# Two-layer spectral attention block on one core: half turns, a 64-wide Gram, x fetched ahead, a new order

## The chip, the cores and the metric

The kernel runs on one core of one Trainium2 chip. The metric is the device time of one launch in microseconds (us), lower is better. The core's engines are TensorE (PE, with its weight loads as PEld), VectorE (DVE), ScalarE (ACT) and GpSimd (POOL), each with a program of its own that it works off strictly in order; SyncE (SP) issues the transfers. The engines wait for one another by semaphores. The work is in float32 throughout.

## What is computed

x has 2 images of 56 channels on a grid of 128 x 128. Two layers of the same form are applied, each with weights of its own. Cut to what matters:

```python
x = x + layer(gn(x))                      # twice; gn: group norm, 32 groups over the last axis
def layer(x):                             # x: 2 x 56 planes of 128 x 128
    xn = inorm(x)                         # mean and variance of each plane
    k, q, v = (fno(xn, W) for W in (K, Q, V))          # 1 -> 8 heads each
    attn = softmax(einsum(q, k) / sqrt(H * W))         # 56 x 56 for each head, over the planes
    out = fno(attn @ v, P)                             # 8 heads -> 1
    att = inorm(out + x);  an = inorm(att)
    h = gelu(inorm(spectral(an, M0)) + skip(an))
    h = inorm(spectral(h, M1)) + skip(h)
    return inorm(h) + att
def spectral(x, w):                       # rfft2, 32 x 16 lowest modes times w, irfft2
def fno(x, w): return spectral(x, w) + skip(x)         # skip: a 1 x 1 product
```

## The kernel before, in words

**Layout.** x lies in `X2`, one image's 56 planes on partitions 0 to 55 (one half of the rows) and 64 to 119 (the other half), with ones on the rows behind them that carry biases into products. For the Fourier transforms the image is turned: TensorE transposes bring a grid column onto the partitions (`turned`), copies put the result into `P[b]`, and `bn_stats` takes sums there. `b` is the image, 0 or 1; each image goes through all steps and both are interleaved.

**Steps of a layer.** `modes` works out the group norm's scale (`gs`, `gv`, `sh`: the statistics `mv` go through a product with `group`), scales `P[b]` in place, multiplies by the discrete Fourier matrix `fw`, turns blocks of 32 x 32 on DVE into `turns`, multiplies again and has the modes `xf`. `gram` multiplies `P[b]` with itself, 128 grid columns summed in PSUM, to a 56 x 56 matrix of all pixels (the skips' part of the scores). `scale_x` scales `X2` itself. `scores`, `softmax`, `values`, `mixes`, `heads` and `norms` are the attention, computed on modes with the products of the heads' weights, which `prepare` makes on the chip (raw weights in `xr`, through `relay` in DRAM, back as `tc16` and `tc20`) and `build` spreads into `WU` and `WT`, `build_m` into `WM`. `norms` ends with `inverse`, the first half of the transform back, to `Z`. `gelu` has 8 pieces of 16 rows for each image: `synthesis` (the second half of the transform) and `mixed` (the skips from `X2` by `Bs`) are summed in PSUM, ACT does Gelu and a Square with a sum, `turn_back` transposes on TensorE, `forward` multiplies by `fw`. `spectrum` is the second spectral product with its norms, a chain of short steps, again ending in `inverse`. `end` does `synthesis` and `mixed` with `Be`, a DVE step (stt) that adds the gelu's result, and adds the layer's input x, fetched again from DRAM into 3 slots of `xr` (`load`, `back`); it writes `store` (layer 0) or `out` (layer 1). For layer 0 it is followed by `turned` for layer 1.

**What sets the order.** The functions only record: each call of an engine becomes a unit of a `_Book`. `play` (lines 211 to 219) issues all units in an order written out by hand in a string, `_ORDER`; `_ENGINES` says for each unit which engine does it (DVE, POOL or ACT, where there is a choice) and `_BANKS` which of the 8 PSUM banks. So almost every instruction has line 218 in the profile, and groups are told by their tiles. SP's transfers, too, stand in that order and each waits at the head of its queue.

**What the change and the prediction touch.** `load_x`, `prepare`, `turned`, `sums` (used by `norms` and `spectrum`), `modes`, `gram`, `mixes`, `turn_back` in `gelu`, `end`, `play`, and the three strings. The Gram's loop before takes the 56 x 56 matrix in two pieces, in column tiles of 32, four of which take turns:

```python
u, v = 32 * (i % 4), 32 * ((i + 2) % 4)
mm(p[u : u + 32, :K], P[b][:, o : o + 32], P[b][:, o : o + K], i < 2, i >= N - 4, tile_position=(0, u))
mm(p[v : v + m, K : K + 28], P[b][:, o + 28 : o + 28 + m], P[b][:, o + 28 : o + K], ...)
```

Of the kernel before, what the change touches and what calls it, by code (L numbers as in the profile page):

```python
# [10 lines left out]
F32 = mybir.dt.float32  # L11
# [11 lines left out]
for _name, _n in (  # L23
    ("ident", N), ("fw", 32), ("group", N), ("raw", 56), ("fh", N), ("gw", N), ("ext", N), ("fold", 64),
    ("low", K), ("high", K), ("count", 2), ("syn", 1), ("same", 32), ("n2", 1), ("power", 1), ("fx", N), ("gh", 2 * N),
):
    _PARTS[_name] = (sum(n for _, n in _PARTS.values()), _n)
# [3 lines left out]
def _constants():  # L31
# [23 lines left out]
    group = (p[:, None] // 4 == p // 4) / 4.0  # L55
    k = np.arange(K)
    ext, fold = np.zeros((N, N)), np.zeros((N, 64))
    for r in range(2):
# [13 lines left out]
        [own, mirror, -mirror, count * dc * N * re, count * dc * N * im, dc * re, dc * im], 1  # L72
    ).reshape(N, 56)
# [6 lines left out]
        "count": np.concatenate([np.full((N, 1), 2.0), -1.0 * (edge2 & (ky2 != 16)[:, None])[:, :1]], 1),  # L80
        "syn": np.where(edge2 & (ky2 == 16)[:, None], 2.0, 1.0)[:, :1],
        "same": (ky2[:, None] == np.arange(32)) * 1.0,
        "low": ((p % 32)[:, None] == k) * (k < 28),
        "power": np.full((N, 1), -0.5),
        "high": ((p % 32)[:, None] + 28 == k) * (k >= 28),
# [3 lines left out]
    return {"all": np.ascontiguousarray(whole, np.float32), "one": np.ones((8, 64 * N), np.float32)}  # L89
# [79 lines left out]
class _Book:  # L169
# [40 lines left out]
    def play(self, order, chosen, at):  # L210
        for n in order:
            u = self.units[n]
            e = chosen.get(n, u.kind[0])
            for ways in u.calls:
                op, args, kw = ways[e]
                args = [self.to_ap(v, at) for v in args]
                kw = {k: self.to_ap(v, at) for k, v in kw.items()}
                getattr(self.engines[e], op)(*args, **kw)  # L218
# [11 lines left out]
def _planned(book):  # L230
# [8 lines left out]
    "734F05000s4s8q4p4K5m3X6l063U7I5h07080a090c0b0e0d0Z020V011011120W170f0X0Y1318031a19141b150p161f1c0l1d1e1g1j0h1h"  # L239
    "2C0i1i2z1n1k1m041l1Y1o210o201X220r1q2A0g1p0u0t0k0v0C1Z0F25233x280q3y240w3z260y270A0E3A3B293C0z2B2a2b3D2c2d0j3E"  # L240
    "3L3I2e2f3O2g3M2h3F2i0m3G3R3N3T3S0B0S0n0H0J0U0K0P8y0Q4x0M0O0I0N0R0L0D0T0x3H3P5O8x4y5N7b7a4z0G2D3Q4A2E2H9c4B2F2G"
    "2K4C2I2L2J4D2M2N2P2O4E2Q2S2R1r2T4G4H2U2V2W1H2X2Y1s2Z9b301v1I1u3J1t1w1J405P1D411x2k2l4V522j1L2p1K1E1z4W581M1G2w"
    "4T1A1N1O2y4U1P1C2q2v1y2m2u573K2x1T2n1Q2r1F4Z1B2t3d3V1R2s1U8C8z1S2o8A321W389e3W1V3c9g3e6i4I3Y4243398D4Y3Z446j3i"
    "4J3g3m3h314L343j3a5Q373o3b3n35335M5R3l5Y36454M4N46474O3f4X3k565U50484P495V4g4a3u5S3t4j5W4b4m3p5T6e4c4d5X3w4n4o"
    "4k5L5Z4v6f4e4l51604w4f5E3v4hir5x5A6g4i595J6hhB4q4Q3s5y3q4R4rgW6a4S5C614u7f626b4t633r5D7d645k556c5K7e5a6d5b5I65"
    "5c66677g685v7h695B6s8B8E5H6t8H5z8F6k5w8K6u6m6Y536r545F8G6p8I6v6q8L8J8M5G8N6E6n6w7k8O6ok26x5d6B6D6y6C5e6F6z5f6A"
    "8P9d8Q6G5g6H8S8R7l9f6K6J5i7c8T5j6I9j9k8U5l6L6M7m7i6N5n7x6Q7j6O6P796R998X7z6S968Y747n6W7591956T92986U8Z9476777B"
    "6V9093j36X787A8V5o5p975q9h5r7C6Z8W9i5s5t709o7y719a7F727D7G7E5u9V7oh17p7qa2h27rgYa97sa37t7uaah0i6h39Wh5gZa4h4ag"
    "9l9m9X7v9n9p9q7wah9r7P9s9t9u9w9v7Qai9x9y9z9A9B7R9C9D9Y7Sab9Z7T9Eadaca0aja1a5aedb7Ha6af8lddde7Ja7dg7Odfa8dhakdc"
    "an7U7Y807V7Zao7W8w827Xauap849Jal7M9Saravam9R7N81aw859Qas837K9Klp7Lax9Naq878688898a9TatayaB9I8c8b8d9O9M8eaC9G8g"  # L250
    "9F9L8faIaD8r8h8j8saz8vaJ8taF8i8u8kkKaAaKaG8oaE8m8paL9U9PbTaH8naM9HaNbYaOaPc5bJaQbKaWh6aRbMaXaTh7bLaYaUbNaSh8aZ"
    "bOh9bPb0aVbQb1bRbSb3b2bWb4bUbXb5bac0c6c7bVb6b7bZc1c2bbbhb8bobcc3c4c8c9cab9cbbpbdcccecdcfcgbqbebiclbjcmbrchcibl"
    "bkcncjckbfbmcqbgbscocrbnbtbucpbvbCbwbDdim7bxdjbydtdkbEbzdudobFbAcCdvdqbGbBdpejcHcOdxdldwesdmdnbHetdsekbIdreyct"
    "ezcveBdydDcudEdCdAdOeAdzcsdBelcwdFeCcxdPdJcyeDczdQdYdGdKcAdLeFdSe9dIcFcBdZdNdMeajsdRcGeGdHe0eHe1cDe2e3cJcEcPcQ"
    "eJcIe4dTcKeOe5eEe8eedVcLdUcMcNegcReKcScTePeIefcUdXcWcYe6cVcXeQdWcZe7eLeRd4d0d5ebeNeMd1eSedeceieud2eheTemf9imd6"
    "d3f8eUd7eVeneoepd9d8eqeWerdaf7f6gXeXfaeveZfbeYjvexflhEfcf5juf4fvewfmfGfgf0fHfnfifwfhf1hahbfQfpfxfofRf3g1fyfdgb"
    "f2fefAgcfBhefkhffSffgkfChdfFglhgfDfzfjhhfEgqhihjg2hkhygyfqhlhshmhzfshvhtgrfrhpftfugshnhugzhqhAfLhohwhHhxiefIfN"
    "hIfMifhrigiIfPihfJiHfKhCfOiLiGg3iiiChDg4ijg5gBhGjCipiNhFiKiAjxgdiFikjyilfTiPjziniojwfVgAjFfUjAiBiOjBfWiMjEjDfX"
    "fYiqg0jGgug6fZisitiuiviJgGgvjtg7gtgKg8gHgwgaiwjHg9iEgLgeixgJgIiyggiziDgCgfjIjJjKjVjLgNghjTgDgmpxpwgOgjjUjMpyiY"
    "jRjNjOgnpzgEgPgijPgxjQgSi9pukSkRjSpvgRgpk1gQgogTk9kFgFk3kagVjWgUk4kbgMk5hJk6jZk7hKhchLk0kljXhMhNhOhPhQi3k8hUi5"  # L260
    "hXi4hRhYi0hVhZhSjYhWi1hTkcici2kdiQiRidkejni7kikjjgkfi8kmibiSjjkgkkjciaknkhiTkqj1jmkoiUkWjfjokpjll2kXksjikrktjk"
    "iVjdiWkuiXjqkUkTiZkxj0kvkwjpjekykVkZkNkLkDkOkAj2kMjrkYkzj4kBl1kQj5l0l3kCl4j6j7kEkPj8j9jhjakIjbl5l6kGl7kJl8lile"
    "ljl9lmlalflbkHlclgldlklhlwlnlolxlqm2llmemlmfmmltlylulIlzmglrlAlvmnlsmhmilBlFlCmjlHlGmomdlDlEmklJmsmplLlKmzlOlN"
    "lMmtmAlPlQlRmqmBlUmClSlTmrmulVmDmvmwlWm8mGmxlXlYmHmalZm0m1mymImbm3m9mcmNmJm4mEmOm5mKmFm6mPmQmLmUmVmRmMmWmSn1mT"
    "mXmYn2n8mZnfn3n4ngn0n5ocn9nhohn6oonin7nao3njnco2nbo5nmo4nnndo6nonpneo7nko8nlnqo9oaobntnrofnuodognAojnvopoqoenH"
    "oiokolnBomnIonorosotounwnJovoxowoyoEozoFnKnxoAoBnCnsnyoCoDoGoJnLnzoHoKnDnEoInFnOnVqBnWqKnXqCqLrlrknPriqDrepArh"
    "nQrgpBrfnRrjpLpCqUqRpVqSpDqWpGq6qXpMpFpWpEpIq7qgpNpHpJqrpKpXpPqhpOqsoVr3nSr7pQnYqirar0nGp0pUp7nMpYnTq0nNnZnUpS"
    "o0pTq1o1pRoMq5q4oNq3pZoOq2oLrcr2oPr6q8r4q9oQqaoRr5qbrdqjqdqloSqfoToUqeoYqkqcqmoWoZqYrbp2oXp8p9qop1p3p4qpp5qqp6"
    "papbpcpdqnpepgpfphpnpipor8qwpjr1pkqZqtqxplpmpqqyqTpppsquprqzqvqEqAptqGqFr9qMrZqQqVs6qHrms7qJqIrts9qNqOs0ruqPs8"
    "rns1rwrzsasbrGs3s2rorAs5s4rvrqrMrBrxrNryrTrCrDrprsrUrErrrFrWrVrOrYrXrHrPrJrQrIrLrRrSrK"  # L270
)
_ENGINES = (
    "ADDDDDDDDDDDDDDDDDDDDDDDDDDDVGGGVGGVVGGGVGGVGVVVGVVGVGGVGPVVVPSVVPSVVPSVVPSVVPSVVPSVVPSVVPSVVPSVVPSVVPSVVPSVVP"
    "SVVPSVVPSVVVGVVGGGGVVGGGGVVGGGVVADDAADDAADDDDDDAAVGVGGGVVVGGGVVVGVVGVGVGGVGVDDADAADADADDDAADDVVVGGGVGVVVVVGVVV"
    "VPVVVGVVPVSPVVPVGPVVGGGPSGDDPSVVPVVVGVSPVSPVVPVGPVVGGGPVGDDPSPPPPPPPPGVSGPVSVVVGVPSGGGGVGGVGVVVVVGVPPPPPPPPGVV"
    "VPVSVVVGVPVGVVGVGVGGGVVGGGGGVGGGPSPSPPSPPVPVVVSVVVPSPSPSPSPSPSPVSPVPVPPPPPSVPSSVVGPVPVPVVVVGVVVPVVVVVVGPVPVVVV"
# [21 lines left out]
def fno_layers(ctx: ExitStack, tc: tile.TileContext, x, out, weights, small, const):  # L298
# [209 lines left out]
    def turned(b, g, L, stats):  # L508
# [17 lines left out]
        for s in range(2):  # L526
            V.bn_stats(stats[:, 2 * g + s, :], dst[:, 448 * s : 448 * s + 448])
# [593 lines left out]
```

## Time and profile before

| | us |
|---|---|
| three runs | 514.27, 510.6, 501.66 |
| median | 510.6 |
| profiled execution | 508.58 |
| its span, first to last instruction | 506.5 |
| busy in the span: PE, PEld | 383.8, 258.3 |
| DVE, ACT, POOL | 357.4, 174.7, 187.7 |
| mean granted TensorE clock | 0.902 |

The profile lists busy time by engine, the span in 40 equal slices (busy share in tenths, the clock that the throttle granted to TensorE in tenths, transfers), the chain of work that ended last, and groups of instructions. A group's line gives output and input by their names, their shapes, the count, busy us and the mean ns of one, and then the idle time of the engine before them and what ended it. "issue" as a releaser is time in which the engine waited for nothing that the profile shows. Matmuls are pipelined, so a mean duration of 0.2 us can go with a pace of tens of ns.

Marks of the stages in the trace before: statistics of the first image complete at 29.4 us, those of the second at 82.9; the first synthesis of layer 0's gelu part at 142.6; its end at 215.4; statistics of layer 1's first image at 265.0, of its second at 324.6; layer 1's gelu from 373.1 to 451.5; the last synthesis from 478.8; the last DVE step before 498.9, then transfers only. The functions of layer 1's first image that need `WU` begin at 284.4.

### The profile page before, as it was taken

The numbers are of one execution on the slowest core, as the hardware profiler recorded it, in microseconds if no ns is written. First come the engines' busy times: TensorE is split into PE (matmuls) and PEld (weight loads), VectorE is DVE, ScalarE is ACT, GpSimd is POOL, SyncE is SP. The second block draws the span as 40 slices with busy tenths as digits, with TensorE's granted clock in tenths as the row PEclk, the third lists the DMA queues.
The fourth block names the chain that finished last, engine by engine and source line by source line (L and its number), as shares of the span: only waits on it lengthen the run. The fifth ranks groups of instructions, "written<-read, shape, count | busy, mean of one in ns | idle before, by whom it ended". The sixth has DMA issues, their size and how long they took to land.

```text
span 506.5 us, 16657 instructions
## 1 busy us (share of the span) xinstructions
PE 383.8 (76%) x7408; PEld 258.3 (51%) x7408; DVE 357.4 (71%) x613; ACT 174.7 (34%) x238; POOL 187.7 (37%) x227
## 2 busy tenths in 40 slices
PE   2434465889899999995686696996999999954590
PEld 1414345368568656554543484756686546532340
DVE  2584299996685776599898859685756655685685
ACT  1410241521283768532003032620246677411000
POOL 0174097883142211144568634245201001113173
PEclk9999585999999999997798877988999999996696
DMA  8975620000002000146645144000000000378655
GB/s 185 235 149 97 138 47 8 1 20 5 14 3 63 7 2 2 39 137 204 214 116 178 32 132 145 3 12 5 3 3 2 1 1 3 105 224 236 191 170 185
DMA packets 27784, 42.00 MB, mean 83 GB/s; under 512 B 10272, under 2 KB 13216, under 8 KB 27680
## 3 DMA queue, kind: packets, MB, share of 16 engines
q1 hardware_dynamic: 25408, 40.49, 29.8%
q8 instruction: 58, 0.95, 0.8%
q10 hardware_dynamic: 2304, 0.44, 0.5%
q14 instruction: 14, 0.11, 0.1%
HBM read 25.48 MB, written 14.97 MB: 80 GB/s over the span
## 4 chain that ended last, share of the span: by engine, by line
PE 54%; DVE 24%; issue 8%; ACT 5%; POOL 3%; DVEq 0%; ACTq 0%; POOLq 0%
PE banks L218 54%; DVE P L218 8%; ACT P L218 3%; DVE WT L218 2%; DVE stats L218 2%; DVE X L218 2%; DVE WU L218 2%; DVE turns L218 1%; DVE dg L218 1%; DVE f L218 1%; DVE M L218 1%; DVE xr L218 1%; DVE vd L218 1%; DVE D L218 1%; DVE sh L218 1%
## 5 line engine op out<-in xcount | busy, mean ns | idle before, releaser
L218 ACT COPY P<-banks 128x896 f32<-128x896 f32 (+4 forms) x64 | 53.3, 856 | 141.8 <-PE banks L218 95.5
L218 PE MATMUL banks<-P 128*32 128x56 f32 (+3 forms) x2656 | 57.1, 220 | 21.7 <-issue 21.0
L218 PEld LDWEIGHTS banks<-P 128*32 128x32 f32 (+1 forms) x2656 | 48.7, 123 | 30.9 <-issue 27.0
L218 PE MATMUL banks<-C,P 32*128 32x128 f32 (+5 forms) x864 | 59.6, 274 | 3.2 <-DVE P L218 1.1
L218 PEld LDWEIGHTS banks<-C,P 32*128 32x128 f32 (+4 forms) x864 | 48.8, 167 | 22.1 <-issue 11.5
L218 POOL TENSOR_TENSOR X<-X,gvr 121x512 f32<-121x512 f32 x35 | 50.5, 1471 | 10.1 <-DVE gvr L218 7.2
L218 DVE SCALAR_TENSOR_TENSOR P<-P,hs,banks 128x1024 f32<-128x1024 f32 x32 | 39.8, 1275 | 14.7 <-PE banks L218 13.2
L218 DVE BATCH_NORM_STATS2 stats<-P 128x6 f32<-128x448 f32 x64 | 36.6, 611 | 18.7 <-ACT P L218 18.6
L218 PE MATMUL banks<-C,X 56*128 56x56 f32 (+1 forms) x384 | 33.0, 290 | 17.6 <-DMA X<-x 9.8
L218 POOL TENSOR_TENSOR X<-P,xr 128x512 f32<-128x512 f32 x22 | 29.3, 1347 | 32.0 <-DMA xr<-x 14.9
L218 ACT ACTIVATE P<-banks 128x1024 f32<-128x1024 f32 x32 | 32.0, 1021 | 22.5 <-PE banks L218 22.4
L218 PEld LDWEIGHTS banks<-C,X 56*128 56x128 f32 (+1 forms) x384 | 28.1, 181 | 22.7 <-issue 6.7
L218 PE MATMUL banks<-P,C 128*32 128x448 f32 (+2 forms) x216 | 29.8, 567 | 11.3 <-DVE P L218 6.2
L218 DVE TENSOR_TENSOR X<-X,gvr 121x512 f32<-121x512 f32 x29 | 32.8, 1157 | 0.8 <-ACT gvr L218 0.8
L218 ACT ACTIVATE banks<-P 128x1024 f32<-128x1024 f32 x32 | 32.9, 1027 | 0.7
L218 PE MATMUL banks<-X,Bs 57*64 57x512 f32 x256 | 33.0, 607 | 0.0
L218 PE MATMUL banks<-xf,WU 64*64 64x56 f32 x1024 | 24.1, 258 | 11.6 <-issue 6.0
L218 PE MATMUL banks<-X,BTx 57*64 57x512 f32 x256 | 32.5, 618 | 0.0
L218 PEld LDWEIGHTS banks<-xf,WU 64*64 64x64 f32 x1024 | 22.1, 170 | 13.8 <-issue 6.9
L218 PE MATMUL banks<-turns,C 128*32 128x224 f32 (+1 forms) x288 | 25.9, 395 | 4.2 <-DVE turns L218 2.9
L218 DVE COPY P<-banks 128x896 f32<-128x896 f32 (+4 forms) x16 | 14.8, 938 | 19.0 <-PE banks L218 19.0
L218 PEld LDWEIGHTS banks<-P,C 128*32 128x32 f32 (+2 forms) x216 | 11.2, 148 | 21.3 <-issue 8.4
(233 smaller groups left out, 645.1 us busy)
## 6 DMA issues: line engine op xcount, KB each, us to landing
X<-x SPq DMA_DIRECT2D x16, 448.0 KB
xr<-x SPq DMA_DIRECT2D x64, 112.0 KB
store<-X SPq DMA_DIRECT2D x32, 224.0 KB
out<-P SPq DMA_DIRECT2D x32, 224.0 KB
xr<-store SPq DMA_DIRECT2D x32, 112.0 KB
X<-store SPq DMA_DIRECT2D x32, 112.0 KB
X<-const_one SPq DMA_DIRECT2D x4, 256.0 KB
xr<-weights SPq DMA_DIRECT2D x4, 144.0 KB
```

The source lines that it names most:

```text
L218: getattr(self.engines[e], op)(*args, **kw)
```

## The change

1. **Turns.** All transposes are now of 56 rows, 16 in a group instead of 8 of 120 rows, and alternate between rows 0 to 55 and 64 to 119 (`turn`). In layer 0's first turns that was so already.
2. **Statistics.** `bn_stats` and `bn_aggr` on DVE go. The copy out of PSUM is an ACT activation with a running sum, and an ACT Square in place in PSUM gives the sum of squares; all 32 groups' copies are on ACT. The product with `group` now takes 16 columns, and one reduction follows.
3. **Gram** in pieces of 64 columns: 128 matmuls in two column tiles instead of 256 in four; one copy out instead of three.
4. **x for the ends** is fetched into 15 slots: 8 in `WU`, 4 in `WT`, 3 in `xr`. Loads of tile n + 15 follow the add of tile n. In the last end (layer 1, second image) x is added by TensorE, a product with the identity summed in PSUM, where POOL and DVE added it before. `WU` and `WT` of layer 1 can be built only when the tiles have been used.
5. **21 idle products** (`idle`) on TensorE that nothing reads: 17 of 128 x 512 and 4 of 128 x 256; 16 stand before and among the first turns.
6. **Ones** in `X2` come from memsets of rows 32 to 63 ahead of the loads of x and a one-row transfer, instead of four transfers of 256 KB.
7. **prepare** handles real and imaginary parts in one instruction, so has fewer and wider ones; all its transfers are on SP (before: SP or ACT).
8. **sums**: two DVE reductions and four matmuls become 18 matmuls of 32 columns, one copy and two small matmuls.
9. **mixes**: 8 matmuls to 128 rows become 16 to 64 rows in two column tiles.
10. **Order, engines, banks** are searched anew. In both layers syntheses of the first image's `end` that stood inside the gelu part now come behind it (two of four in layer 0, all four in layer 1), and the turns of the second image go between the first image's products. On SP, raw weights come ahead of x, and the prepared weights' write to DRAM ahead of the second image.

The core of the diff (the three strings and the constants' layout are left out):

```diff
     def play(self, order, chosen, at):
         for n in order:
+            if n >= len(self.units):
+                self.idle(n - len(self.units))
+                continue
...
+    slots = [t[:, 512 * n : 512 * n + 512] for t, k in ((WU, 8), (WT, 4), (xr, 3)) for n in range(k)]
...
     def load_x(b):
         for g in range(0, 8, 2):
+            fill("VG", X2[32:64, b, 8 * g : 8 * g + 16, :], 1.0)
...
-    for b in range(B):
-        for c in range(2):
-            D.dma_start(out=X2[64 * c + K : 64 * c + 64, b], in_=const["one"].rearrange("p (i w) -> p i w", w=N))
...
-        dma("DA", to, cpt)
+        D.dma_start(out=to, in_=cpt)
...
+    def turn(p, src):
+        for n in range(8):
+            for c in range(2):
+                q = slice(64 * c, 64 * c + K)
+                T.transpose(p[:, c, K * n : K * n + K], src(q, n), ident[q, q], tile_position=(64 * c, 0))
+
+    def turned(b, g, stats):
         p = pair()
...
-                    T.transpose(p[:, s, N * e : N * e + 120], X2[:120, b, i, :], ident[:120, :120])
+        turn(p, lambda q, n: X2[q, b, 8 * g + n, :])
         dst = P[b][:, 896 * g : 896 * g + 896]
...
-        for s in range(2):
-            V.bn_stats(stats[:, 2 * g + s, :], dst[:, 448 * s : 448 * s + 448])
+        v = p[:, :, :448]
+        S.activation(
+            dst.rearrange("p (x c k) -> p c x k", x=8, c=2), v.rearrange("p c (x k) -> p c x k", x=8), AF.Copy,
+            accum_out=stats[:, g : g + 1],
+        )
+        S.activation(v, v, AF.Square, accum_out=stats[:, 8 + g : 9 + g])
...
-    def sums(p, col, of, start, stop, name):
-        r = sbuf(name, N, K)
-        V.tensor_reduce(r, of.rearrange("p (t k) -> p k t", t=8), AX.X, ALU.add)
-        for j, part in enumerate((of[:, :K], r)):
-            mm(p[:K, col : col + 1], part, C["count"][:, 1 - j : 2 - j], start and j == 0, stop and j == 1)
+    def sums(b, *of):
+        p = bank()
+        for n, v in enumerate(of):
+            book.cut()
+            o = slice(K * n, K * n + K)
+            for t in range(8):
+                q = 32 * (t % 4)
+                mm(
+                    p[q : q + 32, o], C["count"][:, :32], v[:, K * t : K * t + K], n == 0 and t < 4, n == 1 and t > 4,
+                    tile_position=(0, q),
+                )
...
-        V.bn_aggr(mv, stats.rearrange("p n s -> p (n s)"))
...
+        mm(p[:, :16], C["group"], stats, True, True)
+        V.tensor_reduce(gs, p[:, :16].rearrange("p (r n) -> p r n", r=2), AX.X, ALU.add)
...
-            u, v = 32 * (i % 4), 32 * ((i + 2) % 4)
-            mm(p[u : u + 32, :K], P[b][:, o : o + 32], P[b][:, o : o + K], i < 2, i >= N - 4, tile_position=(0, u))
-            m = 28 if i == N - 1 else 32
...
+            u, m = 64 * (i % 2), K if i >= N - 2 else 64
+            mm(p[u : u + m, :K], P[b][:, o : o + m], P[b][:, o : o + K], i < 2, i >= N - 2, tile_position=(0, u))
...
-            mm(pb[:, K * t : K * t + K], XT[:K, t, :], BT[:, :K], True, True)
+            for e in range(2):
+                q = slice(64 * e, 64 * e + 64)
+                mm(pb[q, K * t : K * t + K], XT[:K, t, q], BT[:, :K], True, True, tile_position=(0, 64 * e))
...
-                    T.transpose(p[:, r, N * e : N * e + 120], h3[:120, o : o + N], ident[:120, :120])
+            turn(p, lambda q, n: h3[q, N * n : N * n + N])
...
+        if b == 0:
+            for n in range(len(slots)):
+                load(n)
+        elif L == 1:
+            for n in range(16, 32):
+                load(n)
...
+                if ahead:
+                    book.cut()
+                    for r in range(2):
+                        mm(both[v][:, r, :], ident, back(16 * b + 2 * n + r), False, True)
...
-                    tt("GV", dst[:, o], h3[:, o], back(2 * n + r), ALU.add)
                     if not ahead:
-                        load(2 * n + r + 3)
+                        m = 16 * b + 2 * n + r
+                        tt("GV", dst[:, o], h3[:, o], back(m), ALU.add)
+                        if m + len(slots) < (16 if L else 32):
+                            load(m + len(slots))
...
+    def idle(n):
+        k = 4 if n < 8 else 2
+        nc.tensor.matmul(
+            banks[:, n % 8, : N * k].rearrange("p (k m) -> p k m", k=k), lhsT=ident, rhs=_bc(ident, 1, k), start=True,
+            stop=True, skip_group_check=True,
+        )
```

## The prediction

> **What bounds the kernel now.** I read the page's busy slices first, then the chain that ended last, then busy time by stage (windows cut at the marks where one part of the work hands over to the next), and last the timeline of TensorE inside the first Gram matrix.
>
> ```profile
> PE   2434465889899999995686696996999999954590
> DVE  2584299996685776599898859685756655685685
> PEclk9999585999999999997798877988999999996696
> PE 54%; DVE 24%; issue 8%; ACT 5%; POOL 3%; DVEq 0%; ACTq 0%; POOLq 0%
> ```
>
> TensorE is full in two blocks only (the two gelu parts); elsewhere PE and DVE take turns, and the granted clock dips where PE is hungry. 8% of 506.5 us, 40 us, is "issue": PE waited for nothing that the profile shows.
>
> ```profile
> 36.00:58.60 22.60, 9.54 (x529) 7.28 (x530) 7.25 (x23) 0.00 (x0) 7.06 (x23) 0.87 0.57 113
> 58.60:82.90 24.30, 14.80 (x229) 9.99 (x230) 21.96 (x32) 8.96 (x13) 17.30 (x20) 0.71 0.24 46
> 142.60:215.40 72.80, 71.14 (x1042) 46.32 (x1045) 49.57 (x102) 47.99 (x70) 12.66 (x20) 1.00 0.08 21
> 215.40:249.70 34.30, 23.96 (x233) 16.37 (x232) 31.61 (x51) 7.77 (x11) 17.88 (x16) 0.80 0.60 183
> 373.10:451.50 78.40, 75.95 (x1055) 46.54 (x1052) 47.67 (x83) 47.55 (x66) 9.04 (x9) 1.00 0.14 41
> 451.50:478.80 27.30, 10.17 (x72) 6.30 (x73) 17.89 (x31) 2.33 (x5) 6.30 (x7) 0.69 0.76 218
> 478.80:498.90 20.10, 13.96 (x192) 6.93 (x192) 16.86 (x18) 0.00 (x0) 12.86 (x9) 0.85 0.63 190
> ```
>
> Columns: stretch, length, busy us of PE, PEld, DVE, ACT, POOL, clock, DMA share, GB/s. The gelu parts are PE's (98% and 97%). Row 1 is the first Gram, PE 42% busy with nobody ahead of it. After it DVE is the bound (21.96 of 24.30; 31.61 of 34.30 between the layers). The last two rows are the tail, a chain of short DVE steps that leaves PE 37% busy.
>
> ```profile
> 42.41 1.52 PE L218 MATMUL banks<-P 128*32 128x28 f32 x128 [1.23 <-issue]
> 47.78 1.52 PE L218 MATMUL banks<-P 128*32 128x28 f32 x128 [3.86 <-issue]
> 57.27 1.40 PE L218 MATMUL banks<-P 128*32 128x28 f32 x62 [7.97 <-issue]
> ```
>
> 128 matmuls run in 1.52 us (12 ns each), then PE stands still. 128 pairs of weight load and matmul come with one stretch each; the page's instruction queue q8 moved 0.95 MB in 58 packets, 16.4 KB each, and 7408 pairs over 58 packets are 128 pairs. So a gap is the wait for the next packet. Gaps in the four Gram matrices: 13.1 us here, 3.4 in 99 to 128, 6.0 in 275 to 294 and 4.7 in 340 to 346, 27 us in all.
>
> ```profile
> L218 DVE BATCH_NORM_STATS2 stats<-P 128x6 f32<-128x448 f32 x64 | 36.6, 611 | 18.7 <-ACT P L218 18.6
> L218 PE MATMUL banks<-P 128*64 128x56 f32 x512 | 17.3, 223 | 0.6 <-DVE P L218 0.6
> L218 PE MATMUL banks<-turns,C 128*32 128x224 f32 (+1 forms) x288 | 25.9, 395 | 4.2 <-DVE turns L218 2.9
> ```
>
> These price the statistics that go and the 64-wide matmul that comes.
>
> **The parts and their cost.** The rows are of one execution of 508.58 us (span 506.5 and 2.1 around it); the median of the runs shown, 510.6, is 2.0 above it.
>
> 1. Gram. 2048 pairs become 1024 (a float32 product counts two). A 128*64 128x56 pair is busy 17.3 us / 512 = 34 ns, so a Gram is 256 x 34 ns = 8.7 us where 512 x 12 = 6.1 ran. A packet's cycle was 1.52 us and its gap: 2.1 to 3.7 us with few transfers beside it, a mean of 5.9 in the first Gram. 128 pairs of 34 ns take 4.3, so only the first Gram still waits: 2 x 5.9 = 11.8 for 19.2 (-7), the second 8.7 for 9.5 (-1), layer 1's two 17.4 for 22.9 (-5.5). Together -13.5. Bounds: -27 + 10 = -17 if all gaps go, +10 if all stay.
>
> The Trainium skill, "Runtime: NRT & Kernel Launch", Instruction fetch mechanics, says the fetch is prefetched in 16 KiB blocks and hidden behind the issue of instructions. The block size agrees (16.4 KB a packet), the hiding doesn't (gaps of 1.23 to 7.97 us a block); by the page this part would cost +10 us.
>
> 2. Turns. 32 half turns took 1.95 us at 17.82 us, 61 ns each; 16 make 0.98 us. Whole turns of 120 rows were about 110 ns, 8 make 0.88. 48 groups x 0.1 = +5 us of PE at worst, in gelu 32 x 0.1 = +3; at best, with alternating halves overlapping, -1 in all. I take +1.
>
> 3. Statistics. DVE loses 36.6 us of bn_stats, and the 15.8 us of reduces in "sums" (16 x 0.98). ACT gets an accumulating copy and a Square per group: 0.91 + 0.19 + 0.9 + 0.19, about 2.2 us, x32 = 70 us where copies took 32 x 0.9, so +41, 39 of it net. ACT was busy 34%, with 0 to 9 us in the stretches outside gelu; the cover is there, but a turned group now can't go faster than 2.2 us. What it costs if cover is gone: 8 groups x 1.3 = 10 us per half of x.
>
> 4. First loads. The ones come by 8 memsets, not 4 x 256 KB; 9.7 MB become 8.7. At the 191 GB/s of the first 29.4 us that is 45.5 us to the last landing, then two groups on ACT (4.4) and the group product (1.5): the second half's statistics stand at 51.5, not 82.9. The weights' 0.26 MB now go before x: +1.5 us on the first half's 29.4. Preparing weights in half the instructions frees POOL and DVE under both.
>
> 5. Mode-space products for the first half waited for the last WU build at 82.4 us. With eight builds of 1.1 us placed around the second half's statistics they can begin at about 58. From there 60 us passed before (82.4 to 142.6); I keep 63, since ACT and the second half's work press closer. First gelu at 121: **-21.6**.
>
> 6. First gelu. Rows of PE for it sum to 61.9 us in the new order (two of b0's four syntheses, 6.2 us, leave it); at 97% busy 64 for 72.8: **-9**.
>
> 7. Between the layers (215.4 to 373.1, 157.7 us). DVE's bound loses 32 x 0.61 = 19.5 us of statistics and eight reduces (7.8), of which 13 + 2 lay in its full stretch (-10); layer 1's Gram gaps -5.5; the second half's chain, late at 324.6, starts earlier (-8, half of the 15.4 us that stood behind it). Against it the 6.2 us of synthesis and 16 builds of 1.06 us, on two engines 8.5, which before lay under gelu and now wait until the slots of WU and WT that hold x are free; I put half of these on the path. -23.5 + 6.2/2 + 4.3 = -16; with the 34 us of DVE less crowded I take **-18** (ends -27 and +9).
>
> 8. Second gelu: all four syntheses of b0 with their products (12.4 us of PE) leave it: 60.5 us of rows, 64 for 78.4: **-14.4**.
>
> 9. Tail. b0's 12.4 us now fill the 17 us in which PE idled in 451.5 to 478.8; its eight stt of 1.27 us sit on DVE among the chain's steps, +2. In the end of b1, 16 identity products add x: a 128x512 float32 product on the whole array is not in the trace; from below 2 x 0.22 us (128*32 32x448), from above 2 x 0.61 (the mean of a 57*64 512 matmul, its latency in it); I take 0.85, 13.6 us. PE then has 26.5 us where DVE's chain took 20.1, +6.4. POOL's and DVE's adds go: the last step to the end of the span, 7.6, falls by 2. **+6**.
>
> 10. Idle products. 16 lie before and among the first turns, where PE was busy 9 of 29 us: nothing, unless they delay a landed tile, at most 0.9 each. Five others, 3 us in all: **+3**. If they hold the clock at 1, 58.6 to 82.9 (0.71, 14.8 us busy) would save up to 4 us; I count none.
>
> The Trainium skill, "TensorE: Matmul & The Clock Gate", The HAM clock gate, has the clock at half after an idle window of about 3.4 us. The 0.71 and 0.69 stretches agree; by it the idle products are worth up to those 4 us.
>
> Parts 1 to 4 are spent inside the stages 5 to 9. Sum: -21.6 - 9 - 18 - 14.4 + 6 + 3 = -54 on 508.6, 454.6; rounded, and with the median so near, **455 us**.
>
> **Rivals.**
> - *Builds late between the layers.* The last two x tiles sit in WU's first slots, so the scores' weights of layer 1 wait for the last adds of b1, then eight builds on DVE and POOL, both in order. For: DVE 92% busy there, and the last add of x ended at 280.9 us, the scores of layer 1 began at 284.4. Against: with x fetched ahead the adds wait less (POOL stood 2.01 us on a DMA of xr there). Then stage 7 gives +9, not -18: 482 us.
> - *The gaps are not the fetch, and stay.* Part 1 is +10 for -13.5, on the path for some 13 of the 23: 468. For: the first Gram's gaps grow where loads crowd, which more than a fetch could do. Against: the gap comes after 128 pairs each time. (The Trainium skill's "Runtime: NRT & Kernel Launch", Instruction fetch mechanics, is on this rival's side.)
> - *SP's queue.* The prepared weights' write to DRAM stands ahead of x's second half on SP. If DVE ends preparing at 36 rather than 20, those 3.7 MB land at 55 and stage 5 loses 10: 465.
> - *Slower: the fetch stalls move to gelu.* Pairs fall only from 7408 to about 7170, and x is now fetched during both gelu parts: 15 tiles ahead. A packet then waits as in the first Gram, 4.35 us a block in the mean. There are some 20 blocks in the gelu parts; from 13 stalled blocks on nothing is gained, and 15 or more make it over 521; 18 give 533. For: gaps grew from 1.23 to 7.97 beside the loads. Against: 128 pairs take 7 to 9 us in gelu, longer than most gaps.
>
> **How the numbers follow.** Forecast 0.50 (own range 435 to 474), late builds 0.20, gaps stay 0.05, SP 0.07, stalls in gelu 0.18 (of it 0.13 over 2% slower, 0.05 within). 2% is about what a measurement of this kernel tells from no change. Of the late builds 0.02 reach within 2%. Faster 0.80, same 0.07, slower 0.13. The range 430 to 503 leaves out the gelu stalls but for their low end, and a little below.
>
> **What would show it.** DVE busy near 300 us, ACT near 215; "issue" under 5% of the chain; second statistics at about 50 us, first gelu at 121, its length 64, second gelu near 325 to 335 and 64 long; PE over 90% in the last 26 us. Wrong, if gelu shows "issue" gaps beside x's loads, if WU's builds stand on the chain, or if the first gelu starts after 135.

## The result

The changed kernel takes 433.4 us (median of four runs, 431.0 to 434.3) where the kernel before took 509.3 beside it: 0.858 times the time before, with an interval from 0.847 to 0.869. The forecast was 455 us, its range 430 to 503. The profiled execution has a span of 432.0 us at a granted clock of 0.950 (506.5 and 0.902 before). Ratios here and below leave out executions more than 1.5% above the fastest of the same kernel; medians and brackets hold them all.

The page of the changed kernel, the same four lines as before: TensorE, DVE, the granted clock, and the chain that ended last.

```profile
PE   5979889699999999895899999999899999879994
DVE  4716459995767764789779964646857968977542
PEclk9969998899999999999589999999899999995999
PE 69%; DVE 17%; issue 5%; DMA 3%; ACT 3%; POOL 2%; DVEq 0%; ACTq 0%; POOLq 0%
```

The holes in TensorE's row are filled nearly everywhere. Its busy time hardly changed (391.6 us for 383.8); it stood still for 40 us in place of 123. Of the 391.6 us, 25.1 are the idle products. DVE's busy time fell from 357.4 to 296.7, ACT's rose from 174.7 to 206.1.

By stage, the stretches that answer to those shown before (length, then busy us of PE, PEld, DVE, ACT, POOL; the clock, DMA share and GB/s):

```profile
31.00:57.30 26.30, 23.89 (x507) 17.15 (x507) 12.78 (x22) 18.01 (x34) 12.69 (x17) 1.00 0.61 123
119.80:180.10 60.30, 58.72 (x1100) 37.07 (x1100) 40.27 (x88) 45.12 (x64) 25.00 (x38) 1.00 0.15 40
180.10:213.00 32.90, 25.78 (x394) 16.78 (x394) 29.15 (x39) 14.00 (x31) 19.04 (x20) 0.88 0.36 98
309.50:369.00 59.50, 58.03 (x1071) 35.76 (x1067) 46.30 (x79) 42.12 (x60) 18.07 (x20) 1.00 0.13 36
369.00:399.40 30.40, 26.57 (x310) 13.65 (x310) 24.41 (x36) 3.47 (x7) 16.01 (x15) 0.83 0.56 167
399.40:426.60 27.20, 27.14 (x225) 11.30 (x224) 11.70 (x12) 0.00 (x0) 1.48 (x2) 1.00 0.70 206
```

The first row is the stretch of the first Gram, in which TensorE is now busy 91% of the time, with the second image's turns between the Gram's pieces. Rows two and four are the gelu parts, 60 us each and still TensorE's. The chain of the last spectral product (row five) now has 26.6 us of TensorE work beside it, and the last end (row six) is TensorE's alone.

| stage, us | before | after | change | forecast |
|---|---|---|---|---|
| start to first synthesis | 142.6 | 119.8 | -22.8 | -21.6 |
| gelu, layer 0 | 72.8 | 60.3 | -12.5 | -9 |
| between the layers | 157.7 | 129.4 | -28.3 | -18 |
| gelu, layer 1 | 78.4 | 59.5 | -18.9 | -14.4 |
| last chain, end, tail | 55.0 | 63.0 | +8.0 | +6 |
| idle products (beside the stages) | | | | +3 |
| sum | 506.5 | 432.0 | -74.5 | -54 |

### The profile page after: what moved, and what is told of

Same layout as the page of the kernel before. It is cut to its first block, busy times and chain, and to the rows that moved or that the text cites. A ratio compares the mean times of both kernels' runs of the same rounds, so it can differ in the third digit from the quotient of the medians.

```text
span 432.0 us, 16050 instructions
## 1 busy us (share of the span) xinstructions
PE 391.6 (91%) x7138; PEld 252.3 (58%) x7138; DVE 296.7 (69%) x491; ACT 206.1 (48%) x329; POOL 192.2 (45%) x226
## 3 DMA queue, kind: packets, MB, share of 16 engines
q1 hardware_dynamic: 27824, 39.80, 34.8%
## 4 chain that ended last, share of the span: by engine, by line
PE 69%; DVE 17%; issue 5%; DMA 3%; ACT 3%; POOL 2%; DVEq 0%; ACTq 0%; POOLq 0%
PE banks L222 67%; DVE P L222 5%; DVE M L222 2%; PE banks L1073 2%; DVE X L222 2%; DMA X<-x 2%; DVE f L222 2%; POOL P L222 1%; DVE WT L222 1%; DMA sm<-small 1%; ACT P L222 1%; DVE r L222 1%; DVE der L222 1%; DVE D L222 1%; DVE turns L222 1%
## 5 line engine op out<-in xcount | busy, mean ns | idle before, releaser
L222 ACT ACTIVATE P<-banks 128x896 f32<-128x896 f32 (+1 forms) x64 | 61.4, 966 | 46.6 <-PE banks L222 43.8
L222 PE MATMUL banks<-P 128*64 128x56 f32 (+2 forms) x1632 | 63.5, 231 | 1.1 <-POOL xr L222 0.9
L222 PEld LDWEIGHTS banks<-P 128*64 128x64 f32 (+1 forms) x1632 | 55.3, 140 | 15.2 <-issue 11.3
L222 PEld LDWEIGHTS banks<-C,P 56*128 56x128 f32 (+3 forms) x1096 | 38.9, 162 | 19.7 <-issue 10.5
L222 PE MATMUL banks<-C,P 56*128 56x56 f32 (+3 forms) x1096 | 46.6, 255 | 3.4 <-DVE P L222 2.5
L222 ACT COPY P<-banks 128x896 f32<-128x896 f32 (+4 forms) x33 | 29.8, 911 | 34.2 <-PE banks L222 34.1
L222 PE MATMUL banks<-P,C 128*32 128x56 f32 (+3 forms) x344 | 30.0, 395 | 2.6 <-POOL P L222 2.4
L1073 PE MATMUL banks<-C 128*128 128x512 f32 (+1 forms) x42 | 25.1, 731 | 5.7 <-DMA C<-const_all 5.1
L222 PE MATMUL banks<-C,X 56*128 56x56 f32 x512 | 24.0, 246 | 6.2 <-DMA X<-x 3.7
L222 ACT ACTIVATE banks<-banks 128x896 f32<-128x896 f32 x32 | 29.0, 906 | 0.6
L222 DVE TENSOR_TENSOR X<-X,gvr 121x512 f32<-121x512 f32 x26 | 22.8, 896 | 0.0
L1073 PEld LDWEIGHTS banks<-C 128*128 128x128 f32 x42 | 9.2, 244 | 16.9 <-issue 9.1
```

The lines of the kernel that those rows point to most:

```text
L1073: nc.tensor.matmul(banks[:, n % 8, : N * k].rearrange("p (k m) -> p k m", k=k), lhsT=ident, rhs=_bc(ident, 1, k), start=True, stop=True, s ...
```

## The experiments

All times are medians, with the lowest and highest in brackets. The runs were made in three groups, each with the kernel before beside it: the Gram and the turns (kernel before 511.1 us), the idle products and the column steps (507.0), and the rest (505.8). The changed kernel was repeated only in the second group: 433.1 us (430.2 to 435.2), ratio to the kernel before 0.857 (0.853 to 0.862). Differences in us are to that 433.1. For runs of the first and third group they carry the drift from group to group, so the difference by the ratios is given too. Where a gelu part is said to begin or end, its first or last product with `Bs` is meant, about 1 us after its first synthesis.

> The changed kernel once more, beside the next three on the same chip: 431 to 436 us.

**The Gram alone.** In the kernel before, only the Gram is made 64 wide. With it go the steps that served the old pieces: one copy out of PSUM stands for three steps, one product for four. Places in the order that fall away stay empty, so nothing else moves. The loop:

```diff
-            u, v = 32 * (i % 4), 32 * ((i + 2) % 4)
-            mm(p[u : u + 32, :K], P[b][:, o : o + 32], P[b][:, o : o + K], i < 2, i >= N - 4, tile_position=(0, u))
...
+            u, m = 64 * (i % 2), K if i >= N - 2 else 64
+            mm(p[u : u + m, :K], P[b][:, o : o + m], P[b][:, o : o + K], i < 2, i >= N - 2, tile_position=(0, u))
```

> The kernel before with one part of the change alone: the Gram 64 wide (1024 pairs for 2048), order, engines and banks as before. If its gaps are the wait for the next packet of instructions, the four Grams lose 13.5 us of their 51 and most of it is on the path: 497 to 504 us for 510. If the gaps have another cause and stay, the slower pairs (34 ns for 12, half as many) add 10 us: 516 to 521.

Measured: 486.8 us (485.1 to 490.1) against 511.1, ratio 0.955 (0.950 to 0.961). That is -24 us, the side of the fetch theory, and well beyond its 497 to 504. The timeline of TensorE in the same stretch:

```profile
37.76 1.97 PE L226 MATMUL banks<-P 128*64 128x56 f32 x32
41.31 6.85 PE L226 MATMUL banks<-P 128*64 128x56 f32 x224
51.62 1.94 PE L226 MATMUL banks<-C,X 56*128 56x56 f32 x32 [2.83 <-DMA X<-x]
```

224 pairs run without a stop, 31 ns each, in the place where 128 pairs of 12 ns were followed by 1.23, 3.86 and 7.97 us of standing still. The next thing that TensorE waits for is x itself. Over the whole execution the idle time that TensorE's groups put down to "issue" falls from 27.7 to 0.2 us. The packets of the instruction queue q8 go with the pairs: 58 packets for 7408 pairs before, 50 for 6360 here, and 64 for 8186 in the next run, 127 or 128 pairs a packet each time.

So I was wrong to keep a gap in the first Gram. By my cycle (1.52 us of pairs and the gap behind them, so 2.8, 5.4 and 9.5 us), pairs that take 4 us per packet should still have waited 1.4 and 5.5 us, and they didn't wait. How far ahead packets are fetched, and how much the loads slow them, no run shows; during the 224 pairs all transfers together moved 58 GB/s.

The second effect is what stood behind: the product for the second image's statistics came at 68.4 us for 74.6, the first gelu part began at 131.4 for 143.7, and from its end to the second gelu part it was 156.0 us for 167.1, where layer 1's two Grams lie. Together that is more than the -17 that step 1 of the prediction had for all gaps gone; the excess was not taken apart.

**The Gram back.** The changed kernel with four column tiles of 32 again:

```diff
-            u, m = 64 * (i % 2), K if i >= N - 2 else 64
-            mm(p[u : u + m, :K], P[b][:, o : o + m], P[b][:, o : o + K], i < 2, i >= N - 2, tile_position=(0, u))
+            u, v = 32 * (i % 4), 32 * ((i + 2) % 4)
...
```

> The changed kernel with the Gram back in four column tiles of 32 (2048 pairs), all else as changed. Fetch theory: 16 packets of 128 pairs at 2.1 to 3.7 us each for 8 of 4.3, so +8 to +15 us: 441 to 448, with issue gaps back in the Gram stretches. Rival (fetch hidden): 1024 pairs of 34 ns become 2048 of 12 ns, -10 us: 423 to 427.

Measured: 444.2 us (442.9 to 447.6), +11; by the ratios (0.871 for 0.857) +7. The gaps are back, in layer 0 and in layer 1, some of them ahead of what stands behind the Gram's pieces:

```profile
45.15 1.28 PE L232 MATMUL banks<-P 128*32 128x28 f32 x54 [5.69 <-issue]
61.92 0.73 PE L232 MATMUL banks<-P 128*32 128x28 f32 x50 [1.37 <-issue]
252.22 0.21 PE L232 MATMUL banks<-C,X 56*128 56x56 f32 x1 [2.17 <-issue]
265.68 0.33 PE L232 MATMUL banks<-xf,WU 64*64 64x56 f32 x4 [2.72 <-issue]
```

"issue" over all of TensorE's groups is 16.9 us, where the changed kernel has 1.3. The price is 7 to 11 us here and 24 in the kernel before. That half turns and modes' products now lie between the Gram's pieces and give the fetch time would explain the smaller price; no run tests it.

**The turns.** Two runs take the two sides of "alternating halves" apart. The first puts whole transposes of 120 rows back into the gelu parts:

```diff
-            turn(p, lambda q, n: h3[q, N * n : N * n + N])
+            for r in range(2):
+                for e in range(4):
+                    o = 512 * r + N * e
+                    T.transpose(p[:, r, N * e : N * e + 120], h3[:120, o : o + N], ident[:120, :120])
```

> The changed kernel with the gelu parts' turn_back as 8 transposes of 120 rows, not 16 of 56. The trace after shows 16 half turns in 0.64 us of TensorE pace where 8 whole ones took 0.97; 32 groups in two parts that are 97% TensorE make +10 us: 441 to 445. Rival (the order's slack takes it up): 433 to 435.

The second keeps halves but does 8 of one and then 8 of the other:

```diff
-        for n in range(8):
-            for c in range(2):
+        for c in range(2):
+            for n in range(8):
```

> The changed kernel with the 16 half turns of a group done as 8 of one half and then 8 of the other, not alternating. If alternating is what makes them quick (the weight load of one half runs beside the transpose of the other), a half turn goes from 36 to some 60 ns and 48 groups add 10 to 18 us: 443 to 452. If a half turn is quick because it is small, nothing: 432 to 435.

Measured: 443.7 us (439.4 to 445.7) and 443.9 us (442.8 to 445.2), +10.6 and +10.8; by the ratios (0.868 and 0.870 for 0.857) +5 and +6, whose intervals lie clear of the changed kernel's, the first only just. The three forms of one group in the first gelu part, from the changed kernel, from the one with whole turns, and from the one with halves in a row:

```profile
136.00 0.70 PE L222 MATMUL banks<-C,P 56*128 56x56 f32 x16
```

```profile
135.38 1.04 PE L222 MATMUL banks<-C,P 120*128 120x120 f32 x8
```

```profile
136.17 1.00 PE L222 MATMUL banks<-C,P 56*128 56x56 f32 x16
```

Sixteen alternating half turns take 0.70 us, 8 whole ones 1.04, and 16 halves that don't alternate 1.00. So the gain is the alternation: without it, halves are nearly as slow as whole turns. The Trainium skill, "TensorE: Matmul & The Clock Gate", Packing small matmuls, has a weight load run beside products under way only where it goes to other rows of the array. The 0.70 and 1.00 us agree with that. The two gelu parts take 53.4 and 54.3 us in the changed kernel, 57.5 and 58.0 with whole turns (+7.7 together) and 56.3 and 57.0 with halves in a row (+5.5). This is the price of the turns in the gelu parts that the traces show. The rest of the 10.6 came before the first gelu part, which began 4 us later in the profiled execution with whole turns, with nothing changed ahead of it.

**The idle products**, first without the 16 of the first 34 us, then without the five later ones (`count <= 16`):

```diff
             if n >= len(self.units):
-                self.idle(n - len(self.units))
+                count += 1
+                if count > 16:
+                    self.idle(n - len(self.units))
                 continue
```

> The changed kernel without the 16 idle products before and among the first turns (0 to 34 us). If they only warm the clock: the first groups of turns take 1.95 us for 1.21 where TensorE has waited for a load, the last of them already does, and the first Gram and the turns after it start at half clock: +1 to +4 us. If the statistics are ACT's pace (2.2 us a group, last at 30.8) and the loads', nothing: within 1 us. If the idle products stand in the way: -1 to -4 us.

> The changed kernel without the five later idle products, of which three are in the last chain (385.6, 394.4 and 397.3 us). Clock theory: the last end, 27 us of TensorE and nothing ahead of it, starts at half clock for some 3 us: +1.5 to +3 us. Rival (they stand in the way of the last inverse's second pair, which came 1.1 us after the first): -1 to -2 us.

Measured: 435.3 us (430.3 to 438.1) and 431.1 us (429.0 to 432.7) against 433.1. Neither can be told from the changed kernel (ratios to the kernel before 0.859, 0.853 and 0.857, the intervals overlap). The warming of the first turns can be seen, 1.21 us for 32 half turns after idle products and 1.95 after a wait, but loads and ACT set that stretch: ACT's last step on the first image's sums ended at 30.8 us, 3.9 us after TensorE's last turn. For the five later ones the clock theory's gain of 1.5 to 3 us isn't seen. That they harm isn't shown either: from the end of the second gelu part to the end of the span, where four of them stand, it is 66.9 us without them for 67.1, and the 1.6 us that this trace is ahead was won before the first gelu part.

**The statistics.** bn_stats on DVE again, ACT only copies:

```diff
-        S.activation(
-            dst.rearrange("p (x c k) -> p c x k", x=8, c=2), v.rearrange("p c (x k) -> p c x k", x=8), AF.Copy,
-            accum_out=stats[:, g : g + 1],
-        )
-        S.activation(v, v, AF.Square, accum_out=stats[:, 8 + g : 9 + g])
+        copy("SV", dst.rearrange("p (x c k) -> p c x k", x=8, c=2), v.rearrange("p c (x k) -> p c x k", x=8))
+        book.blank("S")
+        for n in range(2):
+            book.also("V", "bn_stats", stats[:, 2 * g + n, :], dst[:, 448 * n : 448 * n + 448])
```

> The changed kernel with the statistics on DVE again: two bn_stats per group in place of ACT's Square (which goes), bn_aggr and one step before the product with group. DVE gets 64 x 0.61 us back. Theory: between the layers DVE is near its limit (29.6 of 31.6 us busy in 219.6 to 251.2), so layer 1's 16 groups add 10 to 20 us, and the first 16, paced by loads, between -2 and +4: 441 to 456. Rival (DVE has the room, ACT's pace was the cost): 428 to 434.

Measured: 450.8 us (450.2 to 450.8), +17.6, inside the first theory's numbers; by the ratios (0.896 for 0.857) +20. DVE is busy 329.9 us for 296.7, ACT 173.0 for 206.1. The first gelu part began 7.5 us later (128.3 for 120.9), and from its last `Bs` product to the second gelu part it was 146.1 us for 136.3, another 9.8.

**The last end.** x added by POOL and DVE, not by identity products:

```diff
-                    for r in range(2):
-                        mm(both[v][:, r, :], ident, back(16 * b + 2 * n + r), False, True)
...
+                        book.also("GV"[r], "tensor_tensor", h3[:, o], h3[:, o], back(16 * b + 2 * n + r), ALU.add)
```

> The changed kernel with x added in the last end by POOL and DVE, one half each, instead of 16 identity products on TensorE. By the rows the last end was 20.1 us and 7.6 after it before, 27.2 and 5.4 with the identity products, so undoing them should win 4 to 5 us: 427 to 430 (the prediction had +6.4 - 2 for this part). Rival: DVE and POOL now start it with a backlog of the first image's adds, and nothing is won: 432 to 437.

Measured: 432.5 us (429.8 to 435.2), ratio 0.860 (0.854 to 0.867), no difference. The last stretch of that run (its last end had begun at 393.1 us), and then its POOL at the end:

```profile
399.40:421.00 21.60, 8.12 (x96) 3.49 (x92) 14.99 (x14) 0.00 (x0) 15.56 (x10) 0.75 0.61 192
```

```profile
399.34 1.27 POOL L230 TENSOR_TENSOR P<-P,WU 128x512 f32<-128x512 f32 x1
402.25 1.26 POOL L230 TENSOR_TENSOR P<-P,WT 128x512 f32<-128x512 f32 x1
406.63 9.12 POOL L230 TENSOR_TENSOR P<-P,X 128x512 f32<-128x512 f32 x5 [0.22 <-issue]
```

From 399.4 us on TensorE has 8.1 us to do and DVE 15. POOL is the last: at 399 us it still adds tiles of the first image (from WU and WT), and then its own half at 1.8 us each. The rival named this backlog. From the start of the last end to the end of the span this trace takes 34.8 us, the changed kernel's 32.7, so here the identity products are worth 2 us. The trace had made that up earlier: its first gelu part began at 116.5 us for 120.9, though nothing is changed ahead of it (the part on DVE behind POOL shows why).

**x in three slots.** The changed kernel with the 3 slots of `xr` only; each load from the fourth tile on is issued behind the add that frees its slot. The order string wasn't made for this: 14 of the 48 tiles are added ahead of their own load, so what is added there is another tile, and those adds wait less than they should.

```diff
-    slots = [t[:, 512 * n : 512 * n + 512] for t, k in ((WU, 8), (WT, 4), (xr, 3)) for n in range(k)]
+    slots = [t[:, 512 * n : 512 * n + 512] for t, k in ((xr, 3),) for n in range(k)]
...
+        if n >= 3:
+            order = [u for u in order if u not in units]
+            k = order.index(book.adds[L, n - 3]) + 1
+            order[k:k] = units
```

> The changed kernel with x for the ends in the 3 slots of xr again: each load from the fourth on stands behind the add that frees its slot, all else as changed (the 12 others' room stays unused). If fetching ahead matters, adds on POOL and DVE wait for loads as before (POOL stood 14.9 us on xr's loads in the trace before) and, as the ends are on the path between the layers: +8 to +25 us. If the adds are off the path: 432 to 436.

Measured: 494.7 us (492.9 to 495.8), +61 (by the ratios, 0.983 for 0.857, +64), far over the 8 to 25 expected. Until the end of the first gelu part nothing differs (its last `Bs` product ends at 176.0 us, 174.3 in the changed kernel). Then POOL adds a tile, waits for a transfer, and adds the next:

```profile
196.54 1.26 POOL L223 TENSOR_TENSOR X<-P,xr 128x512 f32<-128x512 f32 x1 [4.62 <-DMA xr<-x]
200.59 2.48 POOL L223 TENSOR_TENSOR X<-P,xr 128x512 f32<-128x512 f32 x2 [2.79 <-DMA xr<-x]
209.89 1.26 POOL L223 TENSOR_TENSOR X<-P,xr 128x512 f32<-128x512 f32 x1 [6.82 <-DMA xr<-x]
```

From the end of the first gelu part to the second it takes 176.6 us, 136.3 in the changed kernel, and behind the second 86.7 us for 67.1: 40 and 20 of the 61. This shows what fetching ahead is worth to this order, not what 3 slots cost with an order of their own: the kernel before lived with 3, and its POOL stood 14.9 us on loads of xr.

**DVE behind POOL.** In the changed kernel's trace one step on a single column, 128 x 1, takes 10.72 us:

```profile
68.17 1.01 DVE L222 STREAM_TRANSPOSE turns<-banks 128x448 f32<-128x448 f32 x1
69.03 10.72 DVE L222 TENSOR_TENSOR der<-sm 128x1 f32<-128x1 f32 x1
79.68 0.99 DVE L222 STREAM_TRANSPOSE turns<-banks 128x448 f32<-128x448 f32 x1
```

POOL works through just that time without a pause, from 68.9 to 79.7. Others of 0.15 us elsewhere took 3.64 (201.1 us), 1.97 and 1.58.

Not every execution has this wait. In ten of the traces both the column and the step `vd` behind it (56 x 56) are on DVE as in the changed kernel. Five of them have the 10.72 us on the column. Four split it, 6.7 us on the column and 3.3 on `vd` or 4.7 and 5.3. The run with x added by POOL and DVE in the last end has none of it, with the same instructions on both engines (DVE, then POOL):

```profile
68.94 0.16 DVE L230 TENSOR_TENSOR der<-sm 128x1 f32<-128x1 f32 x1
69.82 0.19 DVE L230 TENSOR_SCALAR vd<-C,vc 56x56 f32<-56x56 f32 x1
```

```profile
68.82 4.23 POOL L230 TENSOR_TENSOR WT<-tc,C 128x512 f32<-128x512 f32 x4
73.01 0.72 POOL L230 TENSOR_TENSOR xr<-xr,C 128x256 f32<-128x256 f32 x1
```

There TensorE doesn't wait for `vd`. What decides whether DVE gets in is not shown. The 3.64 us at the second place is steadier: it is 3.64 to 3.66 us in nine of the ten traces.

The edit turns every such product into tensor_scalar, which takes its second column as a scalar operand:

```diff
-        tt("V", r3[:, 1:2], r3[:, 0:1], d["gm1"][:K], ALU.mult)
+        ts("V", r3[:, 1:2], r3[:, 0:1], d["gm1"][:K], None, ALU.mult)
```

> The changed kernel with DVE's small steps on one column done as tensor_scalar, one tensor operand from SBUF and the other as the scalar operand, instead of tensor_tensor with two. In the trace after, such steps of 0.15 us took 10.72 (69.0), 3.64 (201.1), 1.97 and 1.58 us while POOL worked without a gap. If a two-operand step of DVE has to wait until POOL pauses, they fall to 0.15 and the chains behind them win some 3 + 3.5 + 3 us: 423 to 429. If DVE waited for something else (its queue, a semaphore), nothing: 431 to 436.

Measured: 429.3 us (425.7 to 432.2), -3.8; ratio to the kernel before 0.848 (0.843 to 0.853), the changed kernel's 0.857 (0.853 to 0.862). That is just outside the first theory's 423 to 429, and the intervals of the two ratios touch, so the time alone doesn't settle it. In the trace the columns fell to 0.16 and 0.20 us, as the theory said, and from the first gelu part to the second, where the 3.64 us lay, it takes 133.4 us for 136.3. The largest wait moved on to `vd`. DVE, then POOL, of this run:

```profile
68.91 0.16 DVE L222 TENSOR_SCALAR der<-sm 128x1 f32<-128x1 f32 x1
68.96 1.01 DVE L222 STREAM_TRANSPOSE turns<-banks 128x448 f32<-128x448 f32 x1
69.81 9.98 DVE L222 TENSOR_SCALAR vd<-C,vc 56x56 f32<-56x56 f32 x1
79.72 1.86 DVE L222 STREAM_TRANSPOSE turns<-banks 128x448 f32<-128x448 f32 x2
```

```profile
76.53 2.48 POOL L222 TENSOR_TENSOR X<-X,gvr 121x512 f32<-121x512 f32 x2
78.97 0.78 POOL L222 TENSOR_TENSOR xr<-xr 128x288 f32<-128x288 f32 x1
79.83 0.74 POOL L222 TENSOR_TENSOR xr<-xr,sm 128x128 f32<-128x128 f32 x1
```

DVE's step ends at 79.79, in the 0.08 us that POOL rests between 79.75 and 79.83. The Trainium skill, "SBUF — State Buffer", Who interferes with whom, has DVE and GpSimd share one pair of ports as an exclusive lock, which a DVE step takes if it has two inputs in SBUF or runs in a two-port mode, such as tensor_scalar can. The traces agree in part: the column as tensor_scalar passed in both runs that have it so (0.16 and 0.15 us), transposes out of PSUM passed too (1.01 us), and what waited there were two-input steps and the 56 x 56 tensor_scalar. What no run here shows is why DVE was not let in between POOL's instructions for 10 us in nine traces and was in the tenth.

So the last run gives that one step, `vd`, to ACT, which has 1.2 us to do in those 12, and leaves the five later idle products out:

```diff
-        ts("V", vd, ident[:K, :K], vc, None, ALU.mult)
+        book.blank("S")
+        book.also("S", "activation", vd, ident[:K, :K], AF.Copy, scale=vc)
```

> The kernel with columns as tensor_scalar, and besides vd (56 x 56, the step that took 9.98 us at 69.8 us in that run) done on ACT, and without the five later idle products. If DVE's steps wait for a pause of POOL and vd was the only one there that needs the shared way, the wait is gone (DVE free at 71 instead of 79.7) and TensorE, which stood 3.6 us on vd, goes on: 422 to 427. If the wait only moves to the next DVE step, 427 to 430.

Measured: 423.4 us (420.9 to 430.0), ratio to the kernel before 0.842 (0.837 to 0.847); that is under the changed kernel's interval (0.853 to 0.862), so this version beats the changed kernel. From the version with the columns alone (0.843 to 0.853) it is not told apart. DVE in that stretch:

```profile
69.47 1.85 DVE L233 STREAM_TRANSPOSE turns<-banks 128x448 f32<-128x448 f32 x2
73.70 2.93 DVE L233 TENSOR_TENSOR X<-X,gvr 121x512 f32<-121x512 f32 x1 [0.73 <-ACT gvr L233]
76.67 3.92 DVE L233 TENSOR_TENSOR WM<-tc,C 128x512 f32<-128x512 f32 x1
```

The steps on the path get through; two large two-input steps (0.68 us alone) still wait 2.3 and 3.2 us each, now where nothing hangs on them. TensorE's wait on `vd` of 3.60 us is gone, and the first gelu part begins at 117.1 us for 120.0 with the columns alone. Since one trace of the unchanged steps went without the wait too, this one trace doesn't prove that the edit took it away. How much of the 10 us is the columns, how much `vd` and how much the idle products was not taken apart.

## Why the prediction was right, and where it was too small

The direction, the stages and their order came out as forecast; the sum was 20.5 us short of the spans' difference (54 for 74.5). Of that, 10.3 lie between the layers, 8.0 in the two gelu parts and 3 in idle products that cost nothing beside the stages. The 433.4 us lie within the range of 430 to 503, but 1.6 below the 435 to 474 that the prediction gave to its own forecast: most of its mechanisms held, and its sizes were too cautious. The runs take the Gram, the turns, the statistics, the last end's adds, the slots and the idle products one at a time. The first loads, `prepare`, `sums`, `mixes` and the new order have no run of their own, so their share of the 74.5 us is argued and not shown.

- **Gram (step 1).** Right cause, size too small: -13.5 expected, -24 measured alone, +7 to +11 when undone. The terms that failed are the mean cycle of 5.9 us kept for the first Gram, where no gap was left, and the -5.5 for layer 1, where the Gram alone took 11.1 us off between the gelu parts of the kernel before. Rival two (the gaps are not the fetch, and stay) falls with both runs: the gaps went with half the pairs and came back with them. As a reading, the prediction took the chain's "issue" (8%, 40 us) for TensorE's. TensorE's own groups had 27.7 us of it. In the changed kernel the chain still shows 5%, while TensorE's groups have 1.3 us.
- **Turns (step 2).** The worst price: +1 us where it is -7.7 in the gelu parts alone. I took 61 ns for a half turn from a row at 17.8 us that stood behind a wait for a load. The trace before also had 48 of them in 1.70 us at 63.4, 35 ns each, and that was the row to take: no pause ahead of it, as in gelu. This makes most of the 3.5 and 4.5 us by which the two gelu parts were undersized. In the second, 1.6 us more is that its 60.5 us of rows at 97% busy are 62.4, not the 64 I wrote down.
- **Statistics (step 3).** Right: the cover on ACT was there, and DVE's share comes out of the path (+17.6 to +20 when undone). They were not priced apart but inside stages 5 and 7.
- **First loads, start (steps 4 and 5).** The first gelu began at 119.8 for 121, though the second image's statistics came at 57.3, not 51.5: the order puts its turns between the pieces of the Gram, so they end at 53.3, after the loads. Stage 5 as a whole still came within 1.2 us; what made up for the late statistics was not taken apart, so the closeness may be luck.
- **Between the layers (step 7).** -28.3 for -18. The 4.3 us I put on the path for the builds of WU and WT were not there: in the changed kernel TensorE waited 0.0 us ahead of the group that reads WU, in either layer. (Before, it had 11.6 us ahead of it; the 5.6 of them that were for WU fell in layer 0, at 81.3 us.) So the first rival fell. These 4.3 us and the 5.6 by which layer 1's Grams were undersized in the kernel before are about the 10.3 missing here; in the new order the Gram alone changes this stretch by 2 us, so the split stays open. And I gave fetching x ahead no gain at all of its own; the run with three slots shows that this order rests on it.
- **Tail (step 9).** +8 for +6. The identity products took 0.9 to 1.0 us each for the 0.85 estimated. (The 26.5 us written down for TensorE should have been 27.6, the row's 13.96 and 13.6; the last end took 27.2.) Undoing them doesn't win the 4 to 5 us that this sum implies, since POOL's backlog takes their place: I had counted the old end's 20.1 us as if POOL would still be free.
- **Idle products (step 10).** +3 expected beside the stages; without the five later ones the time is 2 us less, not told from none, and the last stretch, where four of them stand, is 0.2 us shorter.
- **Stalls in gelu.** The rival on the other side did not come: "issue" ahead of TensorE's groups is 1.3 us in all (1.1 at 45.3 us, 0.2 at 256.7), none of it in the gelu parts, with x being fetched during both. A packet lasts 7 us there (60.3 us for 1100 pairs), and that is enough. (By its own numbers 15 stalled blocks would have made 520 us, not over 521; it takes 16.)
- **The signs.** DVE's busy time (296.7 us), the first gelu part's start (119.8) and TensorE's share of the last end (27.1 of 27.2 us) came as named. "issue" at 5.1% of the chain missed its 5% narrowly, ACT was at 206 for 215, and the second statistics (57.3 for 50) were late. The second gelu part began at 309.5 for 325 to 335, and both were 60 us long, not 64.

## What to carry to other kernels

A stream of very short TensorE instructions can outrun its fetch (pairs of 12 ns did, of 31 ns did not): fewer, wider matmuls then win although each is slower. The sign to look for is a gap put down to "issue" ahead of TensorE's groups, here after each 128 pairs; the share of "issue" on the chain mixes the engines. Price a small operation from a row without a wait ahead of it, and from a place like the one where it will stand. Before an engine's step of 10 us on one column is taken at its word, look at what the engine beside it does in those 10 us, and whether a second trace has the wait at all.

## What the runs showed of the hardware that I had not expected

- Alternating the two halves of the rows makes a float32 transpose of 56 rows cost 0.70 us for 16, against 1.00 in a row of one half (one group, the only edit being the order of two loops).
- A DVE step of 0.15 us waited 10.72 us while POOL ran without a pause; the same step with one tensor operand passed in 0.16, and `vd` behind it waited 9.98 in its place. In one of ten traces the two-operand step passed in 0.16 as well.
- The clock row can read 1.00 where TensorE runs slowly: 32 half turns behind waits took 1.95 us at 8.3 to 24.3 us of the kernel before under a clock of 1.00, and 1.21 in the changed kernel where idle products ran ahead of them; in the changed kernel the one group of 1.95 us, at 25.0, has 0.50 beside it.
